# A transformer block in float32: where the heads' means are taken out, and in which order the inputs are made

## The chip, the cores and the metric

The kernel runs on one core of a Trainium2 chip. A core has five engines that run side by side: PE (matmuls), DVE (vector work), ACT (activations), POOL (vector work and descriptors of its own DMAs) and SP (DMA issue). The metric is the device time of one execution in microseconds, the median of three runs. Lower is better.

## The reference

The block takes `x` of shape (2, 2048, 576) and a condition of shape (2, 576), with 16 heads of 36 numbers each and a hidden width of 2304. Everything is float32.

```python
mod = silu(c) @ w_ada + b_ada                      # 6 rows of 576 per batch
xn  = ln(x) * (1 + sc_msa) + sh_msa
q, k, v = split(xn @ w_qkv + b_qkv)                # heads of 36
q, k = ln_head(q, qn_g, qn_b), ln_head(k, kn_g, kn_b)
o   = softmax(q @ k.T * 36**-0.5) @ v
x   = x + g_msa * (o @ w_proj + b_proj)
h   = gelu((ln(x) * (1 + sc_mlp) + sh_mlp) @ w1 + b1)
out = x + g_mlp * (h @ w2 + b2)
```

What matters here is `ln_head`: of each head's 36 numbers of q and of k the mean is taken out, then they are divided by their standard deviation. The mean over a head is linear in the product, so it can be taken out of the columns of the weights and of the bias as well.

## The kernel before, in words

**Stages.** After a short start (the condition's product and the first tile's norm), each of the two batches goes through three stages on PE: *inputs* (q, k and v of 16 token tiles of 128), *attention* (8 pairs of heads, 4 blocks of 512 queries, 4 groups of keys, so 128 steps), and *outputs* (the projection and the residual). The MLP of both batches comes last. The function is `block_of_small`; the other branch (`block_of_any`) does not run.

**Inputs.** `inputs` (L975) loops over the tiles. `product` (L1045) makes q, k or v of a tile in one PSUM tile of two banks; there are four such tiles. Sixteen of a product's 20 passes stand at L1053, four at L1055. `biased` (L1058) adds the bias on DVE and frees the PSUM tile. `centred` (L981) takes the heads' means out of q and k: a reduce (L987), a small multiply (L988), a subtract (L989), and then a square on ACT (L994). One tile later `head_scale` (L996) sums the squares (L999), takes the root on ACT and the reciprocal on DVE (L1007), and multiplies on POOL (L1009). Two tiles later `by_feature` (L1017) turns the tile's 32x32 squares on DVE (L1022) into a piece of the buffer `kr`, and four DMAs on SP (L1024) write them so that the tensor `qk` in DRAM has features as rows.

**Reading ahead.** A token tile is loaded on POOL's queue (L911), normed and turned on DVE (L272 to L283, L927), written turned (L932), read back as features (L940, L942) and modulated on ACT (L949) while the tile before it is multiplied. `xnt` has two buffers: the tile in use and the next.

**Gathers for attention.** When enough tiles have been written, `take_q` and `take_k_block` issue gathers from `qk` on SP (L805, L807): the first block of queries after tile 3, keys in five parts that end with tiles 3, 7, 11, 13 and 15 (`key_tiles`, L979). The DVE work on what they bring (`scaled`, L836, and `parted`, L845 and L846) is done at the next call of `by_feature`.

**Last tile.** Tiles 14 and 15 are made in the order q, k, v. The last `by_feature` is called from attention's first step, through the hook `last_inputs_done` (L1362).

**Attention.** `attend` (L1132) has its order of jobs written out in a list `later`: entry i is done i steps from now. A step makes scores (L1150), exponents on ACT (L1154) and values (L1163); DVE adds the values into `ot` (L1211, L1213), which frees their bank. At the second step of a query block the next block's q is scaled, at the third it is parted; in the fourth comes the division (a reciprocal, L1182, and a multiply, L1183). The next pair's keys are gathered on POOL in the second step of the second query block, and their three DVE jobs (`take_k`, L850) follow in the second, third and fourth steps of the third block. From pair 3 on, `residual_begun` (L1263) loads a tile of x in the fourth step of a block, adds a row on POOL (L1272) and stores it.

**Who sets the order.** PE runs in the order in which the program is written; DVE as well from the inputs on. In attention so do POOL and ACT. Everywhere else the order of ACT, POOL and SP is set by the framework's scheduler when the program is built.

**Memory.** `kr` (four pieces of 8 KB a partition) holds squares, turned tiles, scratch for the gathers' work and, as `spare` (L1234), scratch rows of the outputs stage. `qo` takes attention's result.

Of the kernel before, what the change touches and what calls it, by code (L numbers as in the profile page):

```python
# [31 lines left out]
def dit_block(  # L32
# [719 lines left out]
    def block_of_small():  # L752
# [4 lines left out]
        def token_tiles(count, width=C):  # L757
            pool, close = opened("xs", side="right")
            more = [pool.tile([P, width], F32, name=f"xt{i}") for i in range(count - 1)]
            xs.update(pool=pool, tiles=[*more, x_first])  # L760
            return close

        close_xs = token_tiles(3, C + 64)
        outs, close_outs = opened("outs", side="right")
        qo = outs.tile([P, NKC, N], F32, name="qo")
        kv, close_kv = opened("kv")
        kr = kv.tile([P, NQK - NKC, N], F32, name="kr")
# [11 lines left out]
        ended = kr[:, 3, 1280 : 1280 + BLK]  # L779
# [32 lines left out]
        def gains_by_row():  # L812

            at = {i: kr[:, i, 2 * C : 2 * C + P] for i in range(2)}
# [73 lines left out]
        def input_weights(then=lambda t: None):  # L888
            pool, close = opened("wq")
            wq = pool.tile([P, FULL, 3 * C], F32, name="wq")  # L890
            wq4 = pool.tile([P, 3 * C], F32R, name="wq4")
            bq = pool.tile([P, 3 * C], F32, name="bq")
            for f0, n in ((0, HALF), (HALF, HALF), (C, C), (2 * C, C)):
                f = slice(f0, f0 + n)
                nc.sync.dma_start(out=wq[:, :, f], in_=w_qkv[0:512, f].rearrange("(k p) f -> p k f", p=P))
                if f0 == HALF:
                    for w in (slice(0, C), slice(C, 3 * C)):
                        nc.sync.dma_start(out=bq[0:64, w], in_=w_qkv[512:576, w])
                    for w in range(3):
                        w = slice(w * C, (w + 1) * C)  # L900
                        weight_parts(wq4[:, w], bq[0:64, w])
                if f0 == C:
                    then(1)
                    nc.sync.dma_start(out=bq, in_=b_qkv.partition_broadcast(P))
                    then(2)
            return (wq, wq4, bq), close
# [16 lines left out]
        def squares_turned(xt, queue, squares=None):  # L923

            if squares is None:
                squares = xs["pool"].tile([P, C], F32, name="squares", bufs=1)
# [25 lines left out]
        def input_turned(b, t, queue):  # L952
            return tile_turned(tile_loaded(x[b, t * P : (t + 1) * P, :], queue), queue)

        def input_loaded(turned, queue):
            xnt = part_tiles(xs["pool"], P, bufs=2)
            turned_loaded(xnt, slice(0, P), turned, queue)
            return xnt
# [5 lines left out]
        def second_by_feature(rows):  # L964
            xnt = part_tiles(xs["pool"], P, bufs=2)
            t4, t1 = transposed(*rows, True)
# [3 lines left out]
        def first_modulated():  # L970
            xnt = part_tiles(xs["pool"], P, bufs=2)
# [3 lines left out]
        def inputs(b, weights, work, xnt, rows, loaded):  # L975

            wq, wq4, bq = weights
            normed, squares, taken = {}, {}, []
            key_tiles = (0, 4, 8, 12, 14, 16)  # L979

            def centred(both, w0=0, w1=2):  # L981

                part = both[:, w0 * C : w1 * C]
                heads = part.rearrange("p (h d) -> p h d", d=HD)
                n = (w1 - w0) * H
                sums = work.tile([P, 2 * H], F32, name="sums", bufs=2)
                nc.vector.tensor_reduce(sums[:, :n], heads, AX.X, ALU.add)  # L987
                nc.vector.tensor_scalar_mul(sums[:, :n], sums[:, :n], 1.0 / HD)  # L988
                nc.vector.tensor_tensor(  # L989
                    heads, heads, sums[:, :n].unsqueeze(2).to_broadcast([P, n, HD]), ALU.subtract  # L990
                )
                if w0 == 0:
                    squares["sq"] = kr[:, 3, 0 : 2 * C]
                nc.scalar.activation(squares["sq"][:, w0 * C : w1 * C], part, AF.Square)  # L994

            def head_scale(t, both, parts=((0, 2),)):  # L996
                var = work.tile([P, 2 * H], F32, name="var")
                for w0, w1 in parts:
                    nc.vector.tensor_reduce(  # L999
                        var[:, w0 * H : w1 * H],  # L1000
                        squares["sq"][:, w0 * C : w1 * C].rearrange("p (h d) -> p h d", d=HD),
                        AX.X,
                        ALU.add,
                    )
                nc.scalar.activation(var, var, AF.Sqrt, bias=eps5, scale=1.0 / HD)
                inv = work.tile([P, 2 * H], F32, name="inv")
                nc.vector.reciprocal(inv, var)  # L1007
                heads = both.rearrange("p (h d) -> p h d", d=HD)
                nc.gpsimd.tensor_tensor(  # L1009
                    heads, heads, inv.unsqueeze(2).to_broadcast([P, 2 * H, HD]), ALU.mult  # L1010
                )
                normed[t] = both

            qk_rows["dram"] = dram.tile([2 * C, N], F32, name=f"qk{b}")
            by_square = qk_rows["dram"].rearrange("(k d) (t g j) -> t g d k j", d=SQ, g=P // SQ, j=SQ)

            def by_feature(t):  # L1017

                begun = [*taken]
                taken.clear()  # L1020
                squares = kr[:, t % 3, 0 : 2 * C]
                nc.vector.transpose(squares, normed[t])  # L1022
                for g in range(P // SQ):
                    nc.sync.dma_start(  # L1024
                        out=by_square[t, g], in_=squares[g * SQ : (g + 1) * SQ, :].rearrange("p (k j) -> p k j", j=SQ)
# [3 lines left out]
                if t == TPB - 1:  # L1029
                    taken.extend(take_q(0, 0))  # L1030
                if t + 1 in key_tiles:
# [3 lines left out]
            def last():  # L1035

                by_feature(NT - 1)
                left = [*taken]
                taken.clear()
                return left  # L1040

            def next_rows(t):
                return tile_turned(loaded.pop(0), nc.gpsimd) if loaded else input_turned(b, t, nc.gpsimd)

            def product(w, xnt, ps=None, steps=(0, 1)):  # L1045

                ps = ps or s_tile()
                full, parts, _ = xnt
# [9 lines left out]
            def biased(w, ps, t, both):  # L1058
                bias = halves(bq[:, w * C : (w + 1) * C])
                if w < 2:  # L1060
                    nc.vector.tensor_tensor(halves(both[:, w * C : (w + 1) * C]), ps[:, :, :HALF], bias, ALU.add)
# [8 lines left out]

            if b == 0:
                rows = tile_normed(loaded.pop(0))
            before = None
            for t in range(NT - 2):


                both = work.tile([P, 2 * C], F32, name="both", bufs=3)
                turning = b == t == 0
                if turning:
                    q, k = (product(w, xnt, None, (0,)) for w in range(2))  # L1080
                    for w, ps in enumerate((q, k)):
                        product(w, xnt, ps, (1,))
                    ahead = second_by_feature(rows)
                else:
                    ahead = input_loaded(rows, nc.gpsimd)
                    q = product(0, xnt)
                    k = product(1, xnt)
                    input_modulated(b, ahead)
                biased(0, q, t, both)
                rows = next_rows(t + 2)  # L1090
                biased(1, k, t, both)
                if t > 0:
                    head_scale(t - 1, before)
                v = product(2, xnt)
                biased(2, v, t, both)
                if b == 0 and t == 1:
                    gains_by_row()
                if t >= 2:
                    by_feature(t - 2)
                centred(both)  # L1100
                before, xnt = both, ahead


            for t in range(NT - 2, NT):
                both = work.tile([P, 2 * C], F32, name="both", bufs=3)
                if t + 1 < NT:
                    ahead = input_loaded(rows, nc.gpsimd)
                for w in range(3):
                    ps = product(w, xnt)
                    biased(w, ps, t, both)  # L1110
                    if w == 0:
                        head_scale(t - 1, before)

                    if w == (1 if t % 2 == 0 else 0):
                        if t + 1 < NT:
                            input_modulated(b, ahead)
                        by_feature(t - 2)

                    if t == NT - 1 and w < 2:
                        centred(both, w, w + 1)  # L1120
                    if t == NT - 1 and w == 1:
                        head_scale(t, both, ((0, 1), (1, 2)))
                if t + 1 < NT:
                    centred(both)
                before, xnt = both, ahead
            by_feature(NT - 2)

            return last
# [3 lines left out]
        def attend(b, pool, hooks):  # L1132
# [39 lines left out]
            def finish(p, qb, ot):  # L1172
# [8 lines left out]
                def divided():  # L1181
# [3 lines left out]
                    for h in range(2):  # L1185
                        for c, row, d, n in head_rows((2 * p + h) * HD):
                            for r in (row,) if c < FULL else (row, row + 64):
                                nc.sync.dma_start(
                                    out=qo[r : r + n, c, cols], in_=ot[64 * h + d : 64 * h + d + n, :]
# [635 lines left out]
```

## Time and profile before

| What | us |
|---|---|
| median of three runs (3217.92 to 3222.19) | 3219.87 |
| the profiled execution | 3224.0 |
| its span, first to last instruction | 3222.2 |
| PE busy | 3152.4 (98%) |
| DVE busy | 1607.4 (50%) |
| ACT busy | 1475.5 (46%) |
| POOL busy | 660.7 (21%) |
| mean granted PE clock, as a share of full speed | 0.988 |

The profile is one execution, taken by the hardware profiler. Its page gives busy times, the span in 40 slices, the DMA queues, the chain of work that ended last, and groups of like instructions by line. The same trace answers further questions: busy times in stretches that one chooses (*windows*), what one tile's or line's instructions cost (*tile* and *line* views), who waited for whom (*waits*), and the instructions in order of time (*timeline*), where a bracket gives the engine's idle time ahead of an instruction and what ended it. A matmul of float32 operands shows as two passes. Matmuls overlap, so PE's busy time is not a measure of its peak.

By the chain of work that ended last, PE carries 87% of the span, DVE 6%, DMA 3%. In the slices, PE falls below nine tenths only in the first and second.

### The profile page before, as it was taken

How to read it: one execution, taken by the hardware profiler on the slowest of the kernel's cores; microseconds unless marked ns; L12 is line 12 of the kernel's file. 1: busy time of each engine (PE TensorE's matmuls, PEld its weight loads, DVE VectorE, ACT ScalarE, POOL GpSimd, SP SyncE). 2: the span in 40 equal slices, each digit the busy share in tenths (PEclk: the TensorE clock that was granted, in tenths of full speed). 3: DMA queues.
4: the chain of work that ended last, by engine and by line, in shares of the span. 5: the costliest groups of instructions: out<-in, count | busy, mean ns of one | idle time of the engine just before them, and what ended most of it. 6: DMA issues, size and time to landing. Idle time of an engine off the chain costs nothing.

```text
span 3222.2 us, 46882 instructions
## 1 busy us (share of the span) xinstructions
PE 3152.4 (98%) x17548; PEld 1876.1 (58%) x17548; DVE 1607.4 (50%) x2263; ACT 1475.5 (46%) x2841; POOL 660.7 (21%) x927
## 2 busy tenths in 40 slices
PE   7998999999999999999999999999999999999999
PEld 5773333333333787633333333348888888777777
DVE  5774444434444577733444443436566554455454
ACT  2235666666666122357666666652555652000000
POOL 4551000111110354300000111003333320111121
PEclk9998999999999999999999999999999999999999
DMA  5553212222221645521112222137544533333331
GB/s 156 107 113 92 75 35 69 60 75 74 63 82 37 190 97 114 102 57 44 49 45 58 67 71 67 49 98 242 160 131 136 146 107 123 141 132 111 118 103 38
DMA packets 303541, 308.89 MB, mean 96 GB/s; under 512 B 183432, under 2 KB 235848, under 8 KB 301192
## 3 DMA queue, kind: packets, MB, share of 16 engines
q1 hardware_dynamic: 255440, 189.35, 20.5%
q0 software_dynamic: 44320, 110.83, 13.0%
q10 hardware_dynamic: 3544, 5.60, 0.5%
q8 instruction: 141, 2.31, 0.3%
q14 instruction: 96, 0.79, 0.1%
HBM read 191.68 MB, written 103.50 MB: 92 GB/s over the span
## 4 chain that ended last, share of the span: by engine, by line
PE 87%; DVE 6%; DMA 3%; SPq 1%; issue 1%; ACT 0%; POOL 0%; DVEq 0%; POOLq 0%; ACTq 0%
PE b L1163 27%; PE b L1150 18%; PE s L1737 15%; PE m L1578 12%; PE s L1053 7%; PE s L406 3%; PE m L1592 2%; PE one L1578 2%; PE s L1055 1%; DVE den L1182 1%; DMA km<-qk 1%; DVE high L845 1%; DVE both L989 1%; DVE kr L1022 1%; SPq L805 0%
## 5 line engine op out<-in xcount | busy, mean ns | idle before, releaser
L1154 ACT ACTIVATE pt<-b 128x512 f32<-128x512 f32 x2048 | 1058.4, 608 | 517.9 <-PE b L1163 292.7
L1163 PE MATMUL b<-pt,vt 128*64 128x512 f32 x4096 | 942.2, 602 | 0.0
L1163 PEld LDWEIGHTS b<-pt,vt 128*64 128x64 f32 x4096 | 273.5, 137 | 589.0 <-issue 451.9
L1150 PE MATMUL b<-qm,km 32*128 32x512 f32 x4096 | 586.7, 622 | 29.3 <-DVE km L836 11.0
L1150 PE MATMUL b<-qe,ke 16*128 16x512 f32 x2048 | 436.6, 797 | 0.0
L1053 PE MATMUL s<-wq,xnt 128*128 128x288 f32 x1536 | 410.8, 411 | 18.9 <-ACT xnt L949 8.1
L1213 DVE TENSOR_TENSOR ot<-b,ot 128x512 f32<-128x512 f32 x192 | 132.6, 691 | 565.6 <-PE b L1163 565.6
L1150 PEld LDWEIGHTS b<-qm,km 32*128 32x128 f32 x4096 | 199.1, 187 | 311.2 <-ACT pt L1154 209.6
L1737 PE MATMUL s<-ws,as 128*128 128x288 f32 x1440 | 351.8, 406 | 0.0
L1053 PEld LDWEIGHTS s<-wq,xnt 128*128 128x128 f32 x1536 | 284.4, 192 | 83.5 <-ACT xnt L949 14.2
L1737 PEld LDWEIGHTS s<-ws,as 128*128 128x128 f32 x1440 | 273.6, 190 | 75.6
L1182 DVE RECIPROCAL den<-den 128x512 f32<-128x512 f32 x64 | 213.7, 3339 | 11.0 <-DMA den<-den_dram 11.0
L932 POOL DMA_DIRECT2D turned<-squares x220 | 148.2, 679 | 309.1 <-DVE squares L927 280.9
L1578 PE MATMUL m<-xnt,wb 128*128 128x256 f32 x864 | 210.2, 379 | 0.9 <-issue 0.9
L1578 PE MATMUL m<-s,wb 128*128 128x256 f32 x864 | 210.0, 379 | 0.0
L1211 DVE COPY ot<-b 128x512 f32<-128x512 f32 x64 | 44.3, 692 | 327.4 <-PE b L1163 327.4
L1150 PEld LDWEIGHTS b<-qe,ke 16*128 16x128 f32 x2048 | 113.7, 187 | 115.0 <-issue 111.8
L1578 PEld LDWEIGHTS m<-s,wb 128*128 128x128 f32 x864 | 164.2, 190 | 22.3
L1269 POOL DMA_DIRECT2D kr<-in_x_dram x32 | 17.5, 546 | 748.7 <-DVE met L784 748.7
L1578 PEld LDWEIGHTS m<-xnt,wb 128*128 128x128 f32 x864 | 158.9, 190 | 20.3 <-issue 1.3
L1616 ACT ACTIVATE cs<-cs,b_sb 128x512 f32<-128x512 f32 x144 | 98.9, 719 | 114.9 <-DVE cs L1611 95.2
L1737 PE MATMUL s<-ws,hidden 128*128 128x288 f32 x576 | 142.3, 406 | 0.0
(197 smaller groups left out, 2998.2 us busy)
## 6 DMA issues: line engine op xcount, KB each, us to landing
gelu<-cs SPq DMA_DIRECT2D x144, 256.0 KB
hidden<-gelu SPq DMA_DIRECT2D x16, 2304.0 KB
qk<-kr SPq DMA_DIRECT2D x128, 144.0 KB
qm<-qk SPq DMA_DIRECT2D x256, 64.0 KB
den<-den_dram SPq DMA_DIRECT2D x128, 128.0 KB
turned<-squares POOLq DMA_DIRECT2D x220, 72.0 KB, 2.5
xnt<-turned POOLq DMA_DIRECT2D x56, 256.0 KB, 4.0
x_dram<-kr POOLq DMA_DIRECT2D x48, 288.0 KB, 2.4
```

The lines of the kernel that those rows point to most:

```text
L406: nc.tensor.matmul(outs[a], stationary(k, a), moving(k, a), start=(first and k == 0), stop=(not first and k == FULL - 1),)
L932: queue.dma_start(out=by_square[g], in_=squares[g * SQ : (g + 1) * SQ, :].rearrange("p (k j) -> p k j", j=SQ))
L1053: nc.tensor.matmul(out_a, full[:, k, :], wq[:, k, f], start=k == 0, stop=False)
L1150: nc.tensor.matmul(ps, k[r, keys], q[r, :], start=first, stop=not first)
L1154: nc.scalar.activation(pt[:, h, :], banks[2 * c + h], AF.Exp, scale=SCALE)
L1163: nc.tensor.matmul(acc[64 * h : 64 * h + 64, :], vt[:, v0 : v0 + 64], pt[:, h, :], start=pt is pts[0][0], stop=pt is pts[-1][0],)
L1182: nc.vector.reciprocal(den, den)
L1213: nc.vector.tensor_tensor(ot, acc, ot, ALU.add)
L1578: nc.tensor.matmul(out_m[m], wb[:, slot[m], k, f * P : (f + 1) * P], moving[m](k), start=k == 0 and m in (1, 2, 5, 6), stop=k == 1 and m == 1,
L1592: nc.tensor.matmul(out_m[m], wr[w][:, f * P : (f + 1) * P], a[:, i, t * PAIR : (t + 1) * PAIR], start=False, stop=i == 1 and m != 2,)
L1616: nc.scalar.activation(part, part, AF.Gelu, bias=b1_sb[:, g : g + 1])
L1737: nc.tensor.matmul(ms[m], stationary[m][:, f, :], ws[m][:, f, :], start=(f == 0), stop=(f == HF - 1))
```

## The change

The heads' means are taken out of the q and k columns of `w_qkv` and of the bias once, at the start of batch 0; the result is written to DRAM for batch 1. The tile's `centred` is gone; the square on ACT stays (`squared`). In batch 0, v of tiles 0, 1 and 2 is made first, then their q, then the loop with k. Tiles are loaded four ahead, turned three ahead, read back two ahead (`xnt` has three buffers, `squares` two). The last tile's products come in the order k, q, v, and its k is squared, scaled and turned ahead of its q; the hook at attention's first step only hands on the gathers left. `kr` is gone: the squares, the turned tile and the gathers' scratch have buffers of their own; `qo` and the eleven `spare` rows are opened after each batch's inputs, where the inputs' work buffers were. The next pair's keys are gathered a query block earlier and their three jobs are four steps apart. In batch 1's start three token tiles are begun ahead instead of two, and the last outputs stage uses seven spare rows instead of nine rows of its own.

The core of the diff (the memory's moves are left out, as told above):

```diff
+        def centred(part):
+            heads = part.rearrange("p k (h d) -> p k h d", d=HD)
+            sums = xs["pool"].tile([P, FULL, H], F32, name="sums", bufs=1)[: part.shape[0], : part.shape[1], : heads.shape[2]]
+            nc.vector.tensor_reduce(sums, heads, AX.X, ALU.add)
+            nc.vector.tensor_scalar_mul(sums, sums, 1.0 / HD)
+            nc.vector.tensor_tensor(heads, heads, sums.unsqueeze(3).to_broadcast([*heads.shape]), ALU.subtract)
...
+            columns(2 * C, HALF)
+            nc.sync.dma_start(out=raw, in_=w_qkv[512:576, :])
+            columns(2 * C + HALF, HALF)
+            then(1)
+            columns(0, HALF)
+            then(2)
+            columns(HALF, HALF)
+            nc.sync.dma_start(out=bq, in_=b_qkv.partition_broadcast(P))
+            columns(C, HALF)
+            columns(C + HALF, HALF)
+            def made(w):
+                part = slice(w * C, (w + 1) * C)
+                if w < 2:
+                    for a in range(2):
+                        centred(wq[:, :, w * C + a * HALF : w * C + (a + 1) * HALF])
+                    centred(raw[:, part].unsqueeze(1))
+                weight_parts(wq4[:, part], raw[:, part])
...
             if b == 0:
-                rows = tile_normed(loaded.pop(0))
+                made, bias_made, kept = making
+                done, modulated = 3, {0, 1, 2}
+                made(2)
+                rows = {t: tile_normed(loaded.pop(t)) for t in (1, 2)}
+                vs = {0: two_steps(2, 0)}
+                biased(2, vs[0], 0)
+                made(0)
+                xnts[1] = second_by_feature(rows[1])
+                v = product(2, 1)
+                biased(2, v, 1)
+                xnts[2] = second_by_feature(rows[2])
+                made(1)
+                v = product(2, 2)
+                biased(2, v, 2)
+                bias_made()
+                for t in range(done):
+                    q = two_steps(0, t) if t == 0 else product(0, t)
+                    biased(0, q, t)
+            for t in range(NT - 1):
+                begun(t)
+                if t >= done:
+                    q = product(0, t)
+                k = product(1, t)
+                if t >= done:
+                    biased(0, q, t)
+                turned_ahead(t)
+                biased(1, k, t)
                 if t > 0:
-                    head_scale(t - 1, before)
+                    head_scale(t - 1)
+                if t >= done:
+                    v = product(2, t)
+                    biased(2, v, t)
+                if b == 0 and t == 2:
+                    gains_by_row(work)
+                    kept()
                 if t >= 2:
                     by_feature(t - 2)
-                centred(both)
-                before, xnt = both, ahead
+                squared(t)
+                modulated_ahead(t)
...
+            t = NT - 1
+            k, q, v = (product(w, t) for w in (1, 0, 2))
+            head_scale(t - 1)
+            by_feature(t - 2)
+            biased(1, k, t)
+            squared(t, 1, 2)
+            by_feature(t - 1)
+            head_scale(t, 1, 2)
+            by_feature(t, 1, 2)
+            biased(0, q, t)
+            squared(t, 0, 1)
+            biased(2, v, t)
+            head_scale(t, 0, 1)
+            by_feature(t, 0, 1, ready=False)
+            return taken
...
-            behind, later = None, [[] for _ in range(7)]
+            behind, later = None, [[] for _ in range(13)]
...
-                if g == 1 and qb == 1 and p + 1 < NPAIR:
+                if g == 1 and qb == 0 and p + 1 < NPAIR:
                     for i, do in enumerate(take_k(p + 1)):
-                        later[4 + i].append(do)
+                        later[3 + NG * i].append(do)
```

`begun(t)` loads tile t + 4 and reads tile t + 2 back, `turned_ahead(t)` norms and turns tile t + 3, `modulated_ahead(t)` modulates tile t + 1 on ACT; `kept` writes the centred weights and bias to DRAM.

## The prediction

> **What bounds the kernel now.** First the busy row (PE 98%, DVE 50%), then PE by stage, since 98% is a mean. The windows view at the stage borders (columns: stretch, length, busy us of PE, PEld, DVE, ACT, POOL, granted PE clock, DMA share, GB/s):
>
> ```profile
> 19.00:251.40 232.40, 219.46 (x972) 175.77 (x972) 164.81 (x254) 63.49 (x140) 108.99 (x144) 0.97 0.53 113
> 251.40:295.20 43.80, 33.71 (x169) 13.73 (x168) 18.58 (x31) 20.86 (x39) 9.54 (x13) 0.77 0.59 139
> 295.20:1052.20 757.00, 754.43 (x5040) 277.11 (x5036) 313.46 (x398) 513.33 (x993) 71.83 (x106) 1.00 0.22 62
> 1052.20:1125.10 72.90, 72.08 (x321) 54.19 (x322) 42.38 (x73) 6.52 (x17) 29.38 (x48) 1.00 0.70 206
> 1125.10:1346.20 221.10, 214.72 (x962) 172.64 (x962) 162.16 (x238) 59.27 (x128) 107.04 (x140) 0.98 0.50 99
> 1346.20:1394.90 48.70, 34.67 (x169) 15.73 (x168) 19.04 (x29) 20.45 (x38) 9.67 (x12) 0.72 0.62 129
> 2222.30:3222.20 999.90, 993.11 (x4608) 834.51 (x4608) 528.17 (x799) 263.33 (x459) 228.17 (x304) 1.00 0.40 125
> ```
>
> Rows 4 (output projection) and 7 (MLP) are full. Elsewhere I compare with an unbroken PE. In the timeline ten product passes start every 2.205 us; a tile is 60 passes, 13.23 us, a batch 211.7. So the input stages (rows 1, 5) lose 20.7 and 9.4. The hand-overs to attention (rows 2, 6) hold five score steps of 2.40 and three value steps of 3.585, 22.7; they lose 21.1 and 26.0. In attention one step of 5.98 in each of pairs 3 to 6 takes 7.74: eight times 1.76. All of it is some 95 us, the ceiling of any gain.
>
> Who ends the waits (timeline; brackets: idle before, releaser):
>
> ```profile
> 153.60 4.21 PE L1053 MATMUL s<-wq,xnt 128*128 128x288 f32 x8 [5.01 <-ACT xnt L949]
> 256.33 0.69 PE L1150 MATMUL b<-qm,km 32*128 32x512 f32 x1 [3.85 <-DVE both L1061]
> 261.05 1.23 PE L1150 MATMUL b<-qm,km 32*128 32x512 f32 x3 [3.14 <-DVE vt L1064]
> 281.59 1.31 PE L1150 MATMUL b<-qm,km 32*128 32x512 f32 x2 [3.10 <-DVE km L836]
> ```
>
> A tile read too late; the last tile's PSUM banks freed late; its keys late. Behind the first stands DVE, which runs in written order and waits for gathers of q and k, with the next tiles' work queued behind:
>
> ```profile
> 130.90 0.55 DVE L836 TENSOR_SCALAR qm<-qm,gb_at 128x512 f32<-128x512 f32 x1 [6.68 <-DMA qm<-qk]
> 242.97 0.55 DVE L836 TENSOR_SCALAR km<-km,gb_at 64x512 f32<-64x512 f32 x1 [5.06 <-DMA km<-qk]
> ```
>
> A slow attention step, on DVE and on POOL:
>
> ```profile
> 635.39 0.53 DVE L836 TENSOR_SCALAR kr<-ke,gb_at 128x512 f32<-128x512 f32 x1
> 635.95 2.08 DVE L845 TENSOR_SCALAR high<-kr,part 128x512 fp32r<-128x512 f32 x1
> 638.07 0.75 DVE L846 SCALAR_TENSOR_TENSOR ke<-kr,part,high 128x512 fp32r<-128x512 f32 x1
> 638.74 3.35 DVE L1182 RECIPROCAL den<-den 128x512 f32<-128x512 f32 x1
> 642.12 0.69 DVE L1183 TENSOR_TENSOR ot<-ot,den 128x512 f32<-128x512 f32 x1
> 642.73 0.68 DVE L1213 TENSOR_TENSOR ot<-b,ot 128x512 f32<-128x512 f32 x1
> 636.32 1.42 POOL L1272 TENSOR_TENSOR kr<-kr 128x576 f32<-128x576 f32 x1
> ```
>
> k's last third and the reciprocal share one step: 7.4 us of DVE work between two evictions, in a step of 5.98.
>
> **Part 1: the tile's centring goes.** The tile view of `both`:
>
> ```profile
> L987 DVE TENSOR_REDUCE sums<-both x34: 705/1310/1353, 41.7 to 1351.1; 128x32 f32<-128x1152 f32 x30, 128x16 f32<-128x576 f32 x4
> L989 DVE TENSOR_TENSOR both<-both,sums x34: 757/1359/3274, 43.2 to 1352.1; 128x1152 f32<-128x1152 f32 x30, 128x576 f32<-128x576 f32 x4
> ```
>
> With L988 (0.18) 2.85 us a tile. DVE's other work on a tile adds to 7.8 (three evictions 2.2, L999 1.34, L1007 0.35, L1022 1.37, the rows' norm and turn 2.5), so it has 5.4 us of slack in 13.23, where it had 2.6. PE is the bound, so this is worth nothing directly; it and tiles read further ahead let a gather's wait pass. Such a wait (6.7 plus 4.6 of gathered work at 131-136) holds DVE 11.3 us; PE meanwhile fills four PSUM tiles, 17.6 us, and its next tiles are loaded. So the stalls in mid-stage go: in batch 1 the whole 9.4 but 1 for the first tile: **-8.5**.
>
> **Part 2: batch 0's start.** Added: centring of the q and k weights, four halves of 1152 elements a partition (2.85 each), two last-row parts (0.70+0.17+0.76 = 1.63) and two bias parts (1.63): 17.9 us, once. It can't hide behind full tiles: DVE needs, from 19.5 us on, 1.2 (v's split), 4.4 (rows of two tiles), then the bias, which lands near 27 (0.33 MB/us, now ahead of k's columns), then 8.6 (q made: 5.7+1.63+1.2), 8.6 (k made), 3.3, evictions and three turned tiles: about 71 us until three tiles are through, with the small gain matmul behind it on PE. PE has 39.7 us of products in these 52; v of three tiles covers q's centring, q of three covers k's. Before, PE stood at the same three tiles near 66 (19 + 39.7 + 7 lost at 24-40). So the start itself costs +5; what batch 0 lost after that, 20.7-7 = 13.7, falls to 2.5 (the clock after the stall): **-6**. Bounds -13 (no stall) and +6 (reads late too).
>
> **Part 3: hand-over, against last products at T.** Before, DVE freed q and k banks by T+5.0, v by T+9.7. Now k's is early, but q and v stand on DVE behind two gather waits (keys 8-12, keys 12-14) and k's own chain. Steps: v of tile 14 evicted T-12.5; turn 1.4; gather wait 5.1 as at 242.97 and 2.4 of work: T-3.6; scale 2.4, turn 1.4: T+0.2; k evicted and tile 14 turned T+2.6; its write and the next gather, write landing 5.6 after the turn, gather 4.3: T+10; work 1.7, k's half of the variance 1.7, POOL 1.1, half turn 0.7, q and v out: T+17. From v's release PE took 6.75 to its first values (halved clock, as at 261.05-267.8), then 6.0, 6.0 and 6.0 to the fourth step: T+41.7. k's last gather is made by T+31, the scores that want it come at T+33: no wait. 43.8 becomes 41.7, 48.7 becomes 41.7: **-9**. If the scheduler sends the gather of keys 8-12 before the next write, the first wait goes and all is 7 earlier: -23. If another 8 come in: +7. I take the middle since every gather in this trace follows the next write.
>
> **Part 4: the next pair's keys four steps apart.** k's thirds move to the first step of a query block, the reciprocal stays in the last. There remain 0.13+3.35+0.69, 4.2 us, between evictions in 5.98: -8x1.76 = -14.1; and two of these stalls (1931, 2030) are followed by value groups of 5.3 instead of 3.58, -3.4; smaller collisions in pairs 0 to 2, -0.6: **-18**. Here two rules of the Trainium skill speak. "SBUF — State Buffer", section "SBUF: two separate sides": VectorE and GpSimd share a port pair as an exclusive lock. The row agrees (L845 needs 0.49 alone, 2.08 until POOL's 1.42 ended), and it speaks against the change: POOL's add stays in the reciprocal's step, so L1183 may wait up to 1.42. The sum is then 5.6, still under 5.98; the gain stays, with 0.4 to spare. "TensorE: Matmul & The Clock Gate", section "Why this matters for your kernels", warns of gaps over some 3 us only. By it the 0.64 us of PE idling at 1931 costs no clock and this part is 14.7; the trace shows 0.72 of the clock in the 6 us after it, so I take 18.
>
> **Part 5: costed at nothing.** Weights kept in DRAM: 3.25 MB written, 10 us at 0.33 MB/us, on SP near 45-65, where DMA share was 0.1-0.4; uncovered it delays tile 3 by up to 4. Batch 1 loads 5.3 MB instead of 4.9 beneath 72.9 us of projection, and DVE is rid of six weight splits (3.6) there while a third begun tile adds 1.4. `both` and the turned copies in new buffers, output tiles opened late: they overlay memory whose readers ended before; seven spare rows instead of nine: POOL may wait 2.5 for a store, six tiles ahead of need. MLP unchanged.
>
> **Sum.** -8.5-6-9-18 = -41.5 from the profiled execution's 3224.0 us (span 3222.2 and 1.8 around it): 3182.5. It lies 4.1 above the median 3219.87, so the same change gives **3178**.
>
> **Rivals.**
> - *The gather is early*: the SP queue has no work that must precede it. Hand-over -23: 3164. Against: the order at 237.94-241.85 in the trace.
> - *DVE's start and tail eat their parts*: centring shows in full and q/v banks come no earlier: parts 2 and 3 nothing, 3193.
> - *Attention doesn't gain* (the change doesn't do what it says there): the reciprocal's step stays late by the shared port or a gather. 3196. Against: 4.2 of 5.98.
> - *Slower*: at the last tile the SP queue puts both gathers behind other traffic. Banks of q and v, queued on DVE behind them, are freed late, and each us counts in both batches. It decides where gains of 41.5 are spent: 21 us later per batch, T+38 rather than T+17; at T+42 it is 3228. For it: batch 1's last gather landed after 7.65 us. Against: that is the longest.
>
> **Chances.** Main 0.58 (own range 3169-3188), early gather 0.13, start and tail 0.15, attention 0.07, slower 0.04, within 0.2% (6.4 us, what a measurement of this kernel tells from no change) 0.03. Faster: 0.93. The range 3159-3200 takes in the first four and the bounds of parts 2 and 3; below lie early gather with a stall-free start, above the rest.
>
> **What would show it.** Right: no L987 on tiles; stages of about 227, 212.5 and hand-overs near 42; no 7.74 steps; DVE idle on km before q's eviction at the last tile. Wrong: PE waiting on ACT xnt after tile 4, or hand-overs over 50.

## The result and the profile after

| | before | after |
|---|---|---|
| median, us | 3221.03 (4 runs, 3217.92 to 3222.23) | 3189.77 (4 runs, 3187.14 to 3193.61) |
| the profiled execution, us | 3224.0 | 3187.1 |
| its span, us | 3222.2 | 3185.4 |

The ratio is 0.9905, with a 95% interval of 0.9888 to 0.9922: faster by 31 us. (The table ahead of the prediction has the first three of before's four runs.) The prediction said 3178, with a range of 3159 to 3200. The windows view of after, at the borders of the same stages (columns as before: stretch, length, busy us of PE, PEld, DVE, ACT, POOL, granted PE clock, DMA share, GB/s):

```profile
19.02:248.90 229.88, 217.60 (x974) 174.29 (x974) 144.75 (x235) 62.85 (x144) 106.91 (x140) 0.98 0.57 126
248.90:289.60 40.70, 26.34 (x168) 12.16 (x168) 13.59 (x24) 20.22 (x39) 7.36 (x13) 0.79 0.66 149
289.60:1040.40 750.80, 750.75 (x5040) 275.52 (x5036) 308.16 (x402) 512.93 (x993) 71.77 (x106) 1.00 0.23 62
1113.60:1326.70 213.10, 212.06 (x962) 171.20 (x961) 118.55 (x187) 55.83 (x122) 101.52 (x131) 1.00 0.53 106
1326.70:1369.00 42.30, 28.12 (x169) 14.09 (x168) 13.83 (x24) 20.12 (x39) 9.95 (x14) 0.76 0.54 110
1369.00:2112.20 743.20, 743.20 (x4956) 272.84 (x4952) 302.77 (x381) 511.32 (x991) 70.63 (x104) 1.00 0.21 56
```

Rows 1 and 4 are the input stages, 2 and 5 the hand-overs, 3 and 6 attention. Batch 1's inputs and both attention stretches are now full: PE's busy time is within 1.1 us of the length and the clock stands at 1.00. What is left is in batch 0's start and the hand-overs. With the borders read to the hundredth (and batch 1's attention from its fourth value group, as for before):

| Stage | before | after | change | predicted |
|---|---|---|---|---|
| inputs, batch 0 | 232.4 | 229.6 | -2.8 | -6 |
| hand-over, batch 0 | 43.8 | 40.8 | -3.0 | -2.1 |
| attention, batch 0 | 757.0 | 750.7 | -6.3 | } -18 |
| attention, batch 1 | 754.0 | 743.3 | -10.7 | } |
| projection, batch 0 | 72.7 | 73.2 | +0.5 | 0 |
| inputs, batch 1 | 221.3 | 213.2 | -8.2 | -8.5 |
| hand-over, batch 1 | 48.7 | 42.2 | -6.4 | -7.0 |
| sum | | | -36.9 | -41.6 |

The long waits of PE that are left, from the timeline of after (brackets: idle before, releaser; "issue" means that the profile shows no releaser): one at batch 0's start, one in each hand-over.

```profile
72.75 0.98 PE L835 MATMUL s<-gb_rows,sel 128*128 128x4 f32 x4 [9.05 <-issue]
263.26 2.07 PE L1203 MATMUL b<-qm,km 32*128 32x512 f32 x6 [14.37 <-DVE both L1099]
1342.01 1.22 PE L1203 MATMUL b<-qm,km 32*128 32x512 f32 x1 [14.18 <-DVE both L1099]
```

A step of attention that parts the next pair's keys, on DVE and, in the last row, on POOL:

```profile
604.97 0.69 DVE L1266 TENSOR_TENSOR ot<-b,ot 128x512 f32<-128x512 f32 x1 [3.54 <-PE b L1216]
605.64 3.33 DVE L1235 RECIPROCAL den<-den 128x512 f32<-128x512 f32 x1
609.00 0.69 DVE L1236 TENSOR_TENSOR ot<-ot,den 128x512 f32<-128x512 f32 x1
610.96 0.69 DVE L1266 TENSOR_TENSOR ot<-b,ot 128x512 f32<-128x512 f32 x1 [1.26 <-PE b L1216]
612.14 0.49 DVE L852 TENSOR_SCALAR high<-ended,part 128x512 fp32r<-128x512 f32 x1
606.55 1.42 POOL L1323 TENSOR_TENSOR spare<-spare 128x576 f32<-128x576 f32 x1
```

The reciprocal is followed by 1.26 us in which DVE waits for PE, not PE for DVE; the parting that took 2.08 takes 0.49, a step later.

### The profile page after: what moved, and what is told of

It is laid out like the page before. It is cut to its first block, busy times and chain, and to the rows that moved or that the text cites. A ratio compares the mean times of both kernels' runs of the same rounds, so it can differ in the third digit from the quotient of the medians.

```text
span 3185.4 us, 46758 instructions
## 1 busy us (share of the span) xinstructions
PE 3122.8 (98%) x17553; PEld 1865.6 (59%) x17553; DVE 1518.5 (48%) x2182; ACT 1471.6 (46%) x2843; POOL 658.1 (21%) x921
## 4 chain that ended last, share of the span: by engine, by line
PE 92%; DMA 2%; issue 2%; DVE 2%; POOL 1%; SPq 1%; ACT 0%; POOLq 0%; DVEq 0%
PE b L1216 29%; PE b L1203 19%; PE s L1784 15%; PE m L1625 12%; PE s L1085 9%; PE s L406 2%; PE m L1639 2%; PE one L1625 2%; PE s L1087 1%; POOL turned L988 1%; POOL both L1050 1%; DMA xt<-in_x_dram 0%; DMA x_dram<-spare 0%; PE s L417 0%; DVE turned_qk L1063 0%
## 5 line engine op out<-in xcount | busy, mean ns | idle before, releaser
L1203 PE MATMUL b<-qm,km 32*128 32x512 f32 x4096 | 568.9, 618 | 28.6 <-DVE both L1099 28.6
L1203 PE MATMUL b<-qe,ke 16*128 16x512 f32 x2048 | 425.0, 797 | 0.0
L812 POOL DMA_DIRECT2D km<-qk x56 | 27.9, 499 | 571.4 <-PE b L1203 568.9
```

Of the source, the lines that this page charges most:

```text
L1203: nc.tensor.matmul(ps, k[r, keys], q[r, :], start=first, stop=not first)
```

## The experiments

All of them compute the whole block. A hand-over is counted from the last product to the fourth group of values. A median comes with its ratio to the kernel before, measured beside it, and that ratio's 95% interval.

**Again.** The kernel after without an edit, beside the next two and the first on the hand-over:

> The changed kernel itself, again, as the measure for the runs beside it. All theories: 3190 by the median, 31 less than before; inputs 229.6 and 213.2, hand-overs 40.8 and 42.2, the attention stretches 750.7 and 743.3, as in its first profile.

3189.95 (0.9907, 0.9891 to 0.9924); stages 231.6, 40.7, 750.7, 213.1, 43.0 and 743.3. So one profiled execution is only a sample: with the same code there, batch 0's inputs take 229.4 to 231.6 us over the executions here, and batch 1's hand-over 42.0 to 43.0 in four of them and 45.1 to 45.3 in three. Attention and batch 1's inputs repeat to 0.1.

**Attention, two ways.** First, after with the next pair's keys as before the change:

```diff
-            behind, later = None, [[] for _ in range(13)]
+            behind, later = None, [[] for _ in range(7)]
...
-                if g == 1 and qb == 0 and p + 1 < NPAIR:
+                if g == 1 and qb == 1 and p + 1 < NPAIR:
...
-                        later[3 + NG * i].append(do)
+                        later[4 + i].append(do)
```

> The changed kernel with the next pair's key jobs where they were: gathered in the second step of the second query block, done in three steps on end. Theory (part 4 of the prediction): the eight steps of 7.74 come back, the attention stretches grow to about 757 and 754, and the kernel is 17 slower than the changed one. Rival (attention gained because the scratch no longer lies in one buffer): the stretches stay at 750.7 and 743.3, no change.

3203.67 (0.9955, 0.9938 to 0.9971): 13.7 above the repetition. Eight steps of 7.73 or 7.74 came back and attention grew by 9.0 and 7.3 us; the other stages stayed within what repeats show. So part 4 does come from where the keys' jobs stand. Second, the kernel before, with only the residual's row (load, POOL's add, store) moved to a block's first step, where no keys are parted:

```diff
-                (3 + t // NBLK, t % NBLK, 3): lambda t=t: residual_begun(b, t) for t in range(NT + 1)
+                (3 + t // NBLK, t % NBLK, 0): lambda t=t: residual_begun(b, t) for t in range(NT + 1)
```

> The kernel before, with only the residual row's load, add and store moved from the fourth to the first step of a query block; the key jobs stay crowded with the reciprocal. Theory A (the shared port: the multiply by the sign waits for POOL's add, 2.08 instead of 0.49): the multiply is back at 0.49, the steps of 7.74 become about 6.1 as in pairs 0 to 2, and the kernel gains 13 to 17. Theory B (mere crowding of DVE): the steps stay at 7.7, no gain.

3202.93 (0.9949, 0.9933 to 0.9966), 15.8 below the kernel before. Here the keys' last third and the reciprocal still share a step. The timeline of this experiment on DVE, and POOL's add:

```profile
633.52 0.49 DVE L845 TENSOR_SCALAR high<-kr,part 128x512 fp32r<-128x512 f32 x1
634.04 0.75 DVE L846 SCALAR_TENSOR_TENSOR ke<-kr,part,high 128x512 fp32r<-128x512 f32 x1
634.71 3.35 DVE L1182 RECIPROCAL den<-den 128x512 f32<-128x512 f32 x1
638.10 0.69 DVE L1183 TENSOR_TENSOR ot<-ot,den 128x512 f32<-128x512 f32 x1
638.70 0.68 DVE L1213 TENSOR_TENSOR ot<-b,ot 128x512 f32<-128x512 f32 x1
640.30 1.41 POOL L1272 TENSOR_TENSOR kr<-kr 128x576 f32<-128x576 f32 x1
```

and of the one ahead of it, with the keys' jobs back beside the add:

```profile
628.62 0.53 DVE L843 TENSOR_SCALAR ended<-ke,gb_at 128x512 f32<-128x512 f32 x1
629.18 2.08 DVE L852 TENSOR_SCALAR high<-ended,part 128x512 fp32r<-128x512 f32 x1
631.29 0.75 DVE L853 SCALAR_TENSOR_TENSOR ke<-ended,part,high 128x512 fp32r<-128x512 f32 x1
629.55 1.41 POOL L1323 TENSOR_TENSOR spare<-spare 128x576 f32<-128x576 f32 x1
```

With the add elsewhere L845 takes 0.49, and the steps of 7.74 become 6.10: of the 1.76 lost in each, 1.64 was DVE held off by POOL's add, and 0.12 the crowding of jobs. The row's load and store moved along; that it was the add rests on the records of before, where each of the eight such L845 beside an add took 2.07 to 2.09 us and none of the 84 others of its size over 0.49. One moved line gives attention nearly what the change gave it (750.4 and 744.0).

This run also shows before's own spread. Its inputs and hand-overs are before's code, and they took 231.4, 222.3, 42.3 and 46.2 us, where before's profiled execution has 232.4, 221.3, 43.8 and 48.7.

**Batch 0's start, three ways.** PE stands 9.05 us ahead of the small matmul with the gains (L835), whose operand DVE begins to copy at 72.50. First that matmul, with its DVE copies, two tiles later:

```diff
-                if b == 0 and t == 2:
+                if b == 0 and t == 4:
                     gains_by_row(work)
+                if b == 0 and t == 2:
                     kept()
```

> The changed kernel with the small gain matmul (which PE waits for 9.1 behind tile 2's k) moved from tile 2 to tile 4. Theory A (that matmul, behind DVE's queue, is what PE waits for): the 9.1 go and batch 0's inputs fall from 229.6 to about 221. Theory B (tile 3's features are late too: ACT modulates them only after tile 2's square, at 73.2, and PE would stand for them just as long): PE waits about 9 for ACT xnt instead, inputs within 1.5 of 229.6.

3196.61 (one run), inputs of batch 0 235.0. PE waits as long, for tile 3's modulated rows:

```profile
73.40 4.21 PE L1085 MATMUL s<-wq,xnt 128*128 128x288 f32 x8 [10.02 <-ACT xnt L1005]
```

Then tile 3 early as well: turned ahead of the bias's centring, modulated ahead of tile 2's squares.

```diff
+                turned_ahead(0)
                 bias_made()
...
-                turned_ahead(t)
+                if b > 0 or t > 0:
+                    turned_ahead(t)
...
+                if b == 0 and t == 2:
+                    modulated_ahead(t)
+                    modulated.add(t + 1)
                 squared(t)
```

> The changed kernel with the gain matmul at tile 4, tile 3 normed and turned on DVE ahead of the bias's centring, and modulated on ACT ahead of tile 2's square. Theory (the start's stall is tile 3 read late behind DVE's centring and ACT's order, plus the gain matmul): the stall of 9.1 and the half clock after it shrink to under 3, batch 0's inputs come to 219 to 223, 7 to 10 less in all. Rival (DVE is simply full until three tiles are through, so that something else on it is late): inputs stay above 226.

3193.49 (0.9930, 0.9913 to 0.9946), inputs 232.4; PE stands 2.33 behind an eviction and then

```profile
76.48 0.61 PE L1087 MATMUL s<-wq,xnt 128*128 128x288 f32 x1 [7.54 <-POOL xnt L390]
```

So the stage gained nothing, where 219 to 223 was expected. It is the same stall under a third releaser: PE goes on at 72.75, 73.40 and 76.48. All three chains run through DVE's queue. In after, 14.4 us pass on DVE from taking out tile 0's k (58.06) to those copies, while PE is through with its products at 63.7. The weights' centring is only part of why that is late: without it, and with the tile's centring back (the first run on the inputs, below), DVE takes out tile 0's k at 55.11, 2.95 earlier, and PE stands longer. Third, one piece of DVE's delay by itself. In after one normalizing operation takes 3.23 us while POOL scales q and k rows; its neighbours take 0.58. Here the first two tiles' scaling is on DVE:

```diff
+                scaled_by = nc.vector if b == 0 and t < 2 else nc.gpsimd
...
-                nc.gpsimd.tensor_tensor(heads, heads, inv.unsqueeze(2).to_broadcast([P, n, HD]), ALU.mult)
+                scaled_by.tensor_tensor(heads, heads, inv.unsqueeze(2).to_broadcast([P, n, HD]), ALU.mult)
```

> The kernel after, with the rows of q and k of batch 0's first two tiles scaled on VectorE instead of GpSimd (twice, about 1.4 us each on VectorE in place of 2.14 on GpSimd). The step in question is why the start stood 9.05 us where 5.9 was worked out: one normalizing operation on VectorE took 3.23 us at 65.9 where its neighbour took 0.58, while GpSimd scaled rows. If the shared port is the cause, that operation takes about 0.58 us again, VectorE pays 1.4 for the scaling, and TensorE's 9.05 us of standing still become 7 to 8.2. If it waited for something else (its rows, its statistics), it stays near 3.2 us and TensorE stands 9 to 10.5 us. The median should move by less than 3 by both.

The timelines, after first (DVE, then POOL):

```profile
65.90 3.23 DVE L283 TENSOR_SCALAR xt<-xt,mv,rstd 128x576 f32<-128x576 f32 x1
66.66 2.14 POOL L1050 TENSOR_TENSOR both<-both,inv 128x1152 f32<-128x1152 f32 x1
```

```profile
65.50 1.36 DVE L1051 TENSOR_TENSOR both<-both,inv 128x1152 f32<-128x1152 f32 x1
68.39 0.58 DVE L283 TENSOR_SCALAR xt<-xt,mv,rstd 128x576 f32<-128x576 f32 x1
72.46 1.36 DVE L1051 TENSOR_TENSOR both<-both,inv 128x1152 f32<-128x1152 f32 x1
```

The 3.23 is gone, so it was POOL's scaling. But PE stands 9.39: the 2.65 saved came back as two scalings of 1.36, the second of which also lies ahead of the gain matmul; the expectation of 7 to 8.2 had counted one. Median 3194.8 (0.9928, 0.9908 to 0.9948; two runs), 5 above after's, where less than 3 was expected; some 2 to 3 of it are batch 1's hand-over (45.3), which the edit does not touch. This names the delay, not a remedy.

**The hand-over, two ways.** In after, q's and v's banks are freed behind DVE's waits for gathers. First, both evictions ahead of all turning:

```diff
-            by_feature(t - 1)
-            head_scale(t, 1, 2)
-            by_feature(t, 1, 2)
             biased(0, q, t)
             squared(t, 0, 1)
             biased(2, v, t)
+            by_feature(t - 1)
+            head_scale(t, 1, 2)
+            by_feature(t, 1, 2)
```

> The changed kernel with the last tile's q and v taken out of PSUM right after its k, ahead of the waits for the gathers. Theory (part 3: PE waits 14.4 for q's bank because DVE stands in the gather wait): the 14.4 go, PE runs into the missing last keys instead at about 26 after the last product, hand-overs fall from 40.8 and 42.2 to about 35 each, 11 to 13 in all. Rival (the late keys set the end anyway, the banks are a wait in front of a wait): no change, hand-overs 40 to 42.

3187.2 (0.9899, 0.9882 to 0.9915), 2.75 below the repetition; 11 to 13 was expected. The wait of 14.4 is gone (first values 7.6 us after the last product), but the fourth group comes at 40.4 and 39.8, since the keys are late now:

```profile
250.38 1.13 PE L1203 MATMUL b<-qm,km 32*128 32x512 f32 x6 [0.23 <-DVE both L1099]
...
276.73 1.31 PE L1203 MATMUL b<-qm,km 32*128 32x512 f32 x2 [5.46 <-DVE km L843]
```

Second, the same order, and the last tile's k turned without first taking the gather of the keys of tiles 12 and 13 (`by_feature(t - 1, ready=False)`):

> The changed kernel with the last tile's banks freed first, as in e3_banks_first, and the last tile's k scaled, turned and written before DVE waits for the gather of keys 12 and 13. Theory (after the banks, the last keys' chain behind that gather is the limit): the last keys are made some 10 earlier than at 277, hand-overs fall from about 40 to 26 to 32, 18 to 28 less than the changed kernel. Rival (the gathers on SP come in the same order and set the end): hand-overs stay at 38 to 40.

3184.41 (0.9894, 0.9878 to 0.9911), the lowest median of all, though the interval overlaps after's. Hand-overs 37.6 and 40.2, not the 26 to 32 expected; the rival of 38 to 40 came nearer, and the last keys are what PE waits for at 275.53, where some 10 us earlier than 277 was expected. PE's waits, then the two hand-overs in the windows view and two short stretches of the first:

```profile
255.42 2.69 PE L1203 MATMUL b<-qm,km 32*128 32x512 f32 x6 [2.17 <-ACT pt L1207]
...
269.19 3.65 PE L1216 MATMUL b<-pt,vt 128*64 128x512 f32 x16 [1.43 <-ACT pt L1207]
...
275.53 0.82 PE L1203 MATMUL b<-qm,km 32*128 32x512 f32 x2 [1.63 <-DVE km L843]
```

```profile
250.30:287.90 37.60, 31.66 (x171) 14.47 (x170) 13.10 (x24) 22.98 (x41) 7.57 (x13) 0.86 0.54 109
1325.80:1366.10 40.30, 31.74 (x171) 14.04 (x170) 13.15 (x23) 22.76 (x41) 9.92 (x14) 0.83 0.55 115
258.00:260.00 2.00, 2.00 (x15) 1.73 (x10) 0.25 (x1) 1.79 (x4) 0.00 (x0) 0.50 0.12 36
280.00:282.00 2.00, 2.00 (x7) 0.72 (x8) 1.24 (x2) 0.00 (x0) 0.00 (x0) 0.50 0.14 50
```

PE is idle 5.9 us instead of after's 14.4 in batch 0, yet busy 5.3 longer for the same work: its stops are short and scattered, and behind two of them the same passes take longer (2.69 us for six where others take 1.13) at a granted clock of 0.50. The means over the hand-overs mislead here (0.86, and 0.79 in after): after has the half clock too, but for the most part while PE stands.

```profile
255.00:260.00 5.00, 0.00 (x0) 0.00 (x0) 2.42 (x5) 0.14 (x1) 0.00 (x0) 0.50 0.61 100
265.00:268.00 3.00, 3.00 (x23) 2.24 (x17) 1.03 (x2) 2.97 (x6) 2.58 (x4) 0.50 0.36 49
```

In batch 0's hand-over PE ran 10.2 us at half clock in this experiment and 5.0 in after. By estimate from these that is 2.6 of the 5.3; the rest is not explained. So part of the idle time was turned into slow time. That a stop-free hand-over would run at full clock was not tried.

**The inputs, two ways.** Was batch 1's gain DVE's lighter tile, or the rows read further ahead? First, reading ahead kept and the means taken out of each tile again, in `squared` (2.85 us a tile); the weights are left as they are loaded:

```diff
+                sums = work.tile([P, 2 * H], F32, name="sums", bufs=2)[:, :n]
+                nc.vector.tensor_reduce(sums, heads, AX.X, ALU.add)
+                nc.vector.tensor_scalar_mul(sums, sums, 1.0 / HD)
+                nc.vector.tensor_tensor(heads, heads, sums.unsqueeze(2).to_broadcast([P, n, HD]), ALU.subtract)
```

> The changed kernel with the means taken out of each tile's q and k again (reduce, multiply, subtract on DVE before the square) and not out of the weights and the bias; everything else as changed. Theory (reading further ahead carries the gain of the input stage; DVE's slack is worth little): batch 1's inputs stay at 213 to 215, batch 0's start loses its centring and its inputs fall to 220 to 225, hand-overs grow by 3 to 6 each; in sum within 4 of the changed kernel. Rival (the lighter tile is what took the stalls away): batch 1's inputs go back to 218 to 221 and the kernel is over 8 slower.

3204.43 (0.9965, 0.9954 to 0.9977), some 14 above after, where 4 at most was expected. Batch 1's inputs stay at 212.2, but the hand-overs grow to 49.5 and 49.9, and batch 0's inputs do not fall (232.4, PE standing 12.3 ahead of the gain matmul). Second, the weights centred once and the rows modulated one tile ahead and turned two ahead, as before:

```diff
-                if t + 2 < NT and t + 2 not in xnts:
-                    xnts[t + 2] = input_loaded(turned.pop(t + 2), nc.gpsimd)
+                if t + 1 < NT and t + 1 not in xnts:
+                    xnts[t + 1] = input_loaded(turned.pop(t + 1), nc.gpsimd)
...
-                if t + 3 < NT:
-                    turned[t + 3] = tile_turned(loaded.pop(t + 3), nc.gpsimd)
+                if t + 2 < NT and t + 2 in loaded:
+                    turned[t + 2] = tile_turned(loaded.pop(t + 2), nc.gpsimd)
```

(and the loads one tile later to match)

> The kernel after, with each tile's rows modulated one tile ahead of its products and turned two ahead, as before the change (after: two and three); the weights stay centred, so VectorE's tile is still the lighter one. The step in question is the stalls in the middle of the input stages (before: 9.4 us in batch 1, after: about 1). If the reading distance carries that gain, batch 1's input stage goes from 213.1 back to 217 to 221 us, TensorE again waits for the modulated rows in mid-stage, and the median rises by 5 to 14. If VectorE's 2.85 us of slack a tile would have been enough alone, batch 1 stays at 213 to 214.5 us and the median moves by less than 3. The hand-overs should stay within 1.5 us of after's 40.7 and 42.2 by both.

3207.57 (0.9964, 0.9952 to 0.9977), some 18 above after, where 5 to 14 was expected. Batch 1's inputs are 223.4, 1 to 2 more even than before the change, with DVE's light tile; batch 0's are 234.8, and the hand-over of batch 1 is 45.2, as in two other runs. PE's waits for modulated rows in batch 1's inputs:

```profile
1248.01 3.74 PE L1085 MATMUL s<-wq,xnt 128*128 128x288 f32 x8 [4.54 <-ACT xnt L1005]
...
1303.71 2.21 PE L1085 MATMUL s<-wq,xnt 128*128 128x288 f32 x8 [0.98 <-ACT xnt L1005]
```

## Why the prediction was right, and what in it was not

**Part 1 (-8.5, measured -8.2).** The size held, and the stalls behind late modulated rows are gone. Of its two reasons only one carries the gain: reading further ahead. Without it the light tile gives nothing here; with it the heavy tile costs nothing here. What the light tile pays for is the hand-over: with 2.85 us of centring for each of the last tiles it was 7 to 9 us longer. Part 3's steps are written without that centring, but the prediction says of the light tile alone that it is "worth nothing directly".

**Part 2 (-6, measured -2.8).** The smallest part, and the one whose size was off. The centring itself ran as worked out, some 18 us in all from 30.3 to 53.2, with evictions in between:

```profile
L899 DVE TENSOR_REDUCE sums<-wq x4: 1341/1348/1353, 30.3 to 43.0; 128x32 f32<-128x1152 f32 x4
L901 DVE TENSOR_TENSOR wq<-wq,sums x4: 1359/1359/1360, 31.9 to 44.6; 128x1152 f32<-128x1152 f32 x4
```

Two terms were mis-sized, by about 1.6 us each. "About 71 us until three tiles are through" became 72.75. For what follows the prediction had 2.5 us, for the clock; it took 4.1 (176.1 us from there to the last product, where thirteen unbroken tiles take 172.0), in which stand the half clock up to 77.1, the gain matmul itself with 0.9, and a wait of 1.06 at 171.37. In neither term was the 2.65 us by which POOL's scaling stretched one operation of DVE's, in the queue that PE waited for. The prediction weighed that very hold in part 4, and its own line for L989 shows one such operation of 3.27 us where the shortest is 0.76 (it stands at 1347.17 in before's second hand-over, beside POOL's scaling at 1347.68), but it did not look for it in part 2. The hold is more than the start was late, so other items of that sum were taken too high. (The wait of 5.9 us that an expectation above speaks of is not in the prediction, which has 12.3 us lost up to 71.) Over five executions with the same code batch 0's inputs took 230.3 on average and before's 231.9, so the gain is nearer 1.5 than 2.8, with only two executions of before. The bounds, -13 to +6, held it.

**Part 3 (-9, measured -9.4).** Right in order: on SP the write goes ahead of the gather, DVE waits 6.85 us on `km`, then frees q's and v's banks, and PE goes on at once.

```profile
240.59 11.39 SPq L1065 DMA_DIRECT2D qk<-turned_qk  x8
254.01 0.31 SPq L812 DMA_DIRECT2D km<-qk  x1
...
256.89 0.42 DVE L843 TENSOR_SCALAR km<-km,gb_at 64x256 f32<-64x256 f32 x1 [6.85 <-DMA km<-qk]
...
262.49 0.72 DVE L1099 TENSOR_TENSOR both<-s,bq 128x576 f32<-128x576 f32 x1
263.13 0.74 DVE L1102 TENSOR_TENSOR vt<-s,bq 128x576 f32<-128x576 f32 x1
```

Both were out 15 to 16 us after the last product, where 17 was said, and the fourth group came at 40.8 and 42.2, where 41.7 was said. The size of the gain is partly luck: it was taken against one execution of before whose two hand-overs add to 92.4, while before's code in the run with the moved row needs 88.5, and after's code there 82.8 to 86.0 in seven executions. That is 2.5 to 9.6 us of gain, about 6 on average. That the new order alone brings it is not shown: with the tile's centring back, the new order's hand-overs were 49.5 and 49.9, no shorter than before's, and no run has the old order with the light tile. The rival of an early gather fell with the order. What it promised was too much as well, as far as the two experiments stand for it: with the banks' wait wholly away each hand-over shrank by 0.4 to 3.2 us, not by 7, since late keys and slow passes took its place.

**Part 4 (-18, measured -17.0).** All eight slow steps went, 14.1, and with them the slow value groups behind two of those in batch 1 (the difference of the two batches' gains is 4.4, where 3.4 was said). Such slow groups are not certain: when the eight steps came back in the first experiment, one of them was followed by one. One step of 7.15 came up in batch 0, 1.05 above what it took before. The account of the cause was half right: "7.4 us of DVE work in a step of 5.98" counted the 2.08 as work. It was 0.49 of work and a wait for POOL, and without that wait the crowded step takes 6.10. So parting the keys elsewhere was one remedy, and moving POOL's row another. That the change also took the parting out of the step with POOL's add, which is where the gain came from, the prediction did not count; in that its right size was luck. The feared wait of L1183 did not come: the reciprocal covers POOL's whole add.

**The sum.** The stages gave 36.9 of 41.5: 3.2 short in part 2, 1.0 in part 4, 0.5 in the projection, the rest within 0.4. The remaining distance, from 36.9 to 31.3 between the medians, is where the profiled executions lie: before's 3.0 above its median, after's 2.6 below. The prediction took off 4.1 for the first, and could not know the second. By the medians 31.3 of the 41.5 came: the sizes by stage flatter the prediction, in parts 2 and 3 above all. The measured 3189.8 lies 12 above 3178, within its range of 3159 to 3200 but outside the 3169 to 3188 of its main case.

## What to carry to other kernels

When an operation takes four times its usual length, look first at what ran on the neighbouring engine at that moment: moving the one that does not matter may give the whole gain with one line. In an engine that runs in written order, taking away one wait shows the next chain, which three times here was nearly as late; before counting on a wait's full length, work out when the second and third releasers come. And measure the parts of a change apart: the lighter tile and the deeper reading ahead looked like one improvement, and each paid in another stage. Last, profile the kernel before more than once: one execution's stages can be 1 to 2.5 us off each, and a gain counted against them is off by as much.

## What the runs showed of the hardware that was not expected

- Not every DVE operation is held by a POOL operation. A TENSOR_SCALAR went from 0.49 to 2.08 beside an add of 1.42, and one from 0.58 to 3.23 beside a multiply of 2.14; a RECIPROCAL over 128x512 took 3.33 with such an add inside its time and 3.35 without. In the held cases shown DVE's record starts 0.37 to 0.76 us ahead of POOL's and ends 0.3 after it, so that no wait appears, only a longer operation. With tile 3 early, the same normalizing operation began 1.11 us after POOL's, took 1.35 and also ended 0.3 after it. POOL's spans are rough.
- Short stops of PE can be followed by a lower clock. In the last experiment on the hand-over it fell to 0.50 about 1.2 and 1.5 us after PE had gone on from stops of 2.17 and 1.63 us. In attention before the change, a stop of 0.64 us at 1931 was followed by a clock of 0.72 over 6 us, but only two of eight such stops were; why those two is open.
